# A decoder kernel: the last layer's norms and stores inside its steps, the first q and k beside the cross attention

## The chip, the cores and the metric

The kernel runs on one core of a Trainium2 chip. The metric is the device time of one execution in microseconds (us); less is better. Everything is fp32.

## The reference

The input is eight sequences of 256 tokens with 128 features, and a context of the same shape. A state-space block (Mamba style) is followed by a layernorm; then comes one cross attention with 16 heads, residual and layernorm; then six layers of windowed self attention with feed-forward; the result is added to the input of those layers and normalised:

```python
# stage 1 (b: 8, s: 256, d: 128): x1 = layernorm(x + ssm(layernorm(x)))
# stage 2: x2 = layernorm(x1 + cross_attention(layernorm(x1), layernorm(ctx)))
# stage 3, six times:
def attn_layer(x, Wqkv, qs, ksc, Wo):
    q, k, v = split(shift_tokens(x) @ Wqkv)      # 16 heads of 64
    q, k = l2norm(q) * qs, l2norm(k) * ksc
    q, k = rotary(q, scale), rotary(k, 1 / scale)
    return local_attention(q, k, v) @ Wo         # windows of 32, one window back
def ffn_layer(x, g, bln, W1, b1, W2, b2):        # x = shift_tokens(x)
    xn = layernorm(x) * g + bln
    a, gate = split(xn @ W1 + b1)                # 341 wide each
    return a * gelu(gate) @ W2 + b2
# x3 = x2; per layer: x3 += attn_layer(x3); x3 += ffn_layer(x3)
# out = layernorm(x3 + x2)
```

## The kernel before

Activations lie with the 128 features on the partitions. A pair of sequences (512 columns) is the unit of stages 1 and 2 and of the feed-forward; a single sequence (256 columns) is the unit of the self attention.

**Layernorm** (`layernorm_steps`, L101 to L138) works across partitions, so PE takes the means: one matmul with a matrix of 1/128 gives the mean spread over all partitions (ln_mu, L104); DVE subtracts (ln_xc, L108); ACT squares (ln_sq, L110); four small matmuls give the variance of each token as one column for each 128 tokens (ln_var, L115); ACT computes the inverse root by Ln and Exp on those four columns (ln_rs); four matmuls spread it over the partitions again (ln_bc, L128); DVE multiplies (L135, or L137 and L138 with gain and bias). It is a generator: a caller can run it in pieces between other work. In `fine` form it yields after each matmul group.

**Order of the work.** DVE, ACT, POOL and the DMA-issuing SP get their orders from a scheduler, starting from program order. In stage 3 PE's order is the program's own (`manual_schedule`). ACT's table for Ln and Exp is loaded again after each gelu (`load_table`, L93 in the profile), and what needs it is held behind that load (`with_table`, L89).

**Pools.** Tiles come from pools; the program opens a new pool for a stage when that of the stage before is closed. Unless told otherwise, the first use of a new pool's tile waits until the old pool that lay in its place is free as a whole.

**Stage 1** (0 to 383 us) runs the state-space scan over four pairs. **Stage 2** (383 to 684 us) loops over four pairs, and in each over 16 groups of heads: scores (s_ps, L514), clip (DVE w, L520), exp (ACT w), sums, and products with v (o_ps, L533). Beside pair p run the layernorms and projections of pair p+1 (`project`), one piece for each iteration; beside pair 3 runs nothing. At a pair's end come y_ps (L566), the residual r (L570) and the layernorm into x2.

**Stage 3** (from 684 us) starts by loading constants (rot, mask), clearing the padded buffers of k (kz, on POOL) and of v (three vz, on DVE), and loading weights: three thirds of wqkv, the scale rows from which DVE makes the rotary tables (`load_table3`, L610 and L616), wo, w1 and w2. Then it runs 48 steps, six layers by eight sequences. The list `slots` says what PE does in one step `run(n)`, for sequence n and, ahead of it, for n+1, n+2 and n+3: `shift` copies the input with the shifted half (xs, L654 and L655); `query_key` makes q or k of half a sequence (qk_ps L663; square L675; products with the tables qk L682 and rb L683; the two adds on POOL L686; sum of squares L687); `root` and `normalise` scale it (L706); `turn` transposes it and puts it down as qT or kz (L713 to L725); `value` copies v, from where DMAs place it in vz (L744); `scores` (L760 to L774), `weigh`, `add_weights`, `turn_weights` (pT_ps, L791), `attend` (L803), `turn_output` (L822) and `project_out` (y_ps, L835; x, L840) do the attention. The first two calls, `run(-2)` and `run(-1)`, fill this pipeline.

The feed-forward of a pair (`feed_forward`, L847 to L896) starts once both its sequences are through. Its pieces run in the "ff" slots of the next two steps. Of the eight "ff" slots in the list, a step n uses those whose number is n % 2; the others pass empty:

```python
if f == "ff":
    if k == n % 2:
        next(ff, None)
```

After step 47 follow the rest of its attention (`project_out`), the feed-forward of pair 3, and then, for the four pairs one after the other, the sum with x2 (L949), the layernorm, and `store` (four transposes st_ps L161, a copy st_o L163, a DMA).

## Time and profile before

| | |
|---|---|
| median of 3 runs | 2500.81 us (2500.76 to 2501.01) |
| the profiled execution itself | 2499.94 us |
| its span in the trace | 2498.2 us |
| busy share of the span: PE, DVE, ACT, POOL | 92%, 72%, 59%, 57% |
| mean granted clock of PE | 0.969 |

The busy share is a mean over stages with different limits. The page cuts the span into 40 slices of 62.5 us and gives the busy share of each in tenths; "PEclk" is the granted clock in tenths. PE reads 6 to 8 in stage 1 (slices 1 to 6), 9 in stage 2 with 8 at its end (slice 11), 7 where stage 3 begins, 9 through its steps, and 6 in the last slice. DVE reads 7 to 8 through the steps of stage 3.

Three views are used below. The windows give busy time by engine for a stretch of the span. The chain of waits follows the work that ended last back through what released it, printed in order of time. The timeline lists the instructions of a stretch. A number such as "x8" is the count of instructions in a group; "L128" is a line of the kernel.

### The profile page before, as it was taken

To read this page: it belongs to the slowest core of one execution; us is meant where nothing else is said; L and a number is where in the kernel's file an instruction comes from. 1 tells how busy PE (TensorE), PEld (TensorE's weight loads), DVE (VectorE), ACT (ScalarE), POOL (GpSimd) and SP (SyncE) were. 2 spreads that over 40 slices of the span, in tenths; PEclk is the share of its full clock that TensorE was granted. 3 is DMA by queue.
4 is the path that set the end of the run, shared out by engine and by line. 5 is a ranking of instruction groups with operands and counts; after the bars stand their busy time and mean duration, and the time that the engine had idled before them with its cause. 6 is when DMAs were issued, how large, how long until landed. Compare 5 with 4: busy or idle time off the path is not lost.

```text
span 2498.2 us, 54483 instructions
## 1 busy us (share of the span) xinstructions
PE 2310.4 (92%) x21378; PEld 1456.9 (58%) x21378; DVE 1795.9 (72%) x2661; ACT 1462.7 (59%) x2400; POOL 1432.0 (57%) x1180
## 2 busy tenths in 40 slices
PE   7688789999879999999999999999999999999996
PEld 3233235554446666666666666666666666666664
DVE  4788874444477777777777778777777877777762
ACT  4444444444446666666666666666666666666652
POOL 3889882222367665665656656666655666656630
PEclk9898899999979999999999999999999999999997
DMA  4444430000032223222222223222232223222220
GB/s 125 96 112 108 100 76 5 5 1 1 1 111 65 56 64 72 68 62 59 71 65 69 60 56 82 65 66 56 64 73 62 68 54 75 56 56 56 58 56 17
DMA packets 437963, 154.62 MB, mean 62 GB/s; under 512 B 401295, under 2 KB 417549, under 8 KB 437581
## 3 DMA queue, kind: packets, MB, share of 16 engines
q1 hardware_dynamic: 437708, 151.14, 25.0%
q8 instruction: 171, 2.80, 0.5%
q14 instruction: 84, 0.68, 0.1%
HBM read 55.33 MB, written 1.31 MB: 23 GB/s over the span
## 4 chain that ended last, share of the span: by engine, by line
PE 43%; DVE 32%; ACT 14%; POOL 4%; issue 3%; DMA 2%; SPq 1%; ACTq 0%; DVEq 0%; POOLq 0%
DVE qk L682 6%; DVE rb L683 6%; PE qk_ps L663 6%; DVE ss L687 6%; PE f_ps L869 3%; PE o_ps L803 3%; DVE on L810 3%; PE qkT_ps L713 3%; PE f_ps L894 2%; ACT sq L675 2%; PE s_ps L514 2%; PE o_ps L533 2%; DVE m L423 2%; POOL mc L425 2%; PE y_ps L835 2%
## 5 line engine op out<-in xcount | busy, mean ns | idle before, releaser
L686 POOL TENSOR_TENSOR qk<-qk,rb 128x512 f32<-128x512 f32 x384 | 481.0, 1274 | 434.4 <-DVE rb L683 288.3
L706 POOL TENSOR_TENSOR qk<-qk,rn 128x1024 f32<-128x1024 f32 x192 | 369.3, 1924 | 31.9 <-ACT rn L89 29.4
L682 DVE TENSOR_TENSOR qk<-qk_ps,tab 128x1024 f32<-128x1024 f32 x192 | 234.9, 1223 | 207.3 <-ACT sq L675 207.3
L663 PE MATMUL qk_ps<-wqkv,xs 128*128 128x512 f32 x768 | 373.7, 610 | 7.8 <-issue 3.1
L774 POOL TENSOR_TENSOR pw<-pw,mx 128x512 f32<-128x512 f32 x192 | 200.5, 1044 | 160.4 <-DVE mx L773 106.7
L725 ACT COPY kz<-qkT_ps 64x1024 f32<-64x1024 f32 x192 | 193.4, 1007 | 119.5 <-PE qkT_ps L713 117.5
L803 PE MATMUL o_ps<-vz,pT 128*32 128x128 f32 x6144 | 207.5, 276 | 29.7 <-ACT pT L795 27.1
L687 DVE TENSOR_REDUCE ss<-sq 128x16 f32<-128x1024 f32 x192 | 232.0, 1208 | 4.0 <-ACT sq L675 4.0
L683 DVE TENSOR_TENSOR rb<-qk_ps,tab 128x1024 f32<-128x1024 f32 x192 | 233.1, 1214 | 1.5 <-POOL qk L686 1.5
L783 DVE TENSOR_REDUCE mx<-pw 128x8 f32<-128x512 f32 x192 | 130.7, 681 | 140.9 <-ACT pw L89 138.7
L720 ACT COPY qT<-qkT_ps 128x1024 f32<-128x1024 f32 x96 | 97.2, 1013 | 218.7 <-PE qkT_ps L713 218.2
L803 PEld LDWEIGHTS o_ps<-vz,pT 128*32 128x32 f32 x6144 | 156.0, 109 | 118.3 <-ACT pT L795 107.2
L675 ACT ACTIVATE sq<-qk_ps 128x1024 f32<-128x1024 f32 x192 | 195.5, 1018 | 44.2 <-PE qk_ps L663 39.4
L713 PE MATMUL qkT_ps<-ident,qk 128*128 128x128 f32 x1536 | 211.1, 281 | 6.8 <-POOL qk L706 4.1
L523 POOL TENSOR_TENSOR ws<-w 128x512 f32<-128x512 f32 x64 | 81.4, 1272 | 216.5 <-ACT w L89 138.7
L760 PE MATMUL s_ps<-kz,qT 128*32 128x128 f32 x6144 | 203.1, 273 | 0.0
L406 PE MATMUL y<-mc,ident 128*128 128x512 f32 x256 | 153.3, 707 | 49.0 <-POOL mc L425 47.8
L663 PEld LDWEIGHTS qk_ps<-wqkv,xs 128*128 128x128 f32 x768 | 134.6, 195 | 106.3 <-issue 103.0
L713 PEld LDWEIGHTS qkT_ps<-ident,qk 128*128 128x128 f32 x1536 | 166.0, 142 | 47.8 <-issue 41.3
L835 PE MATMUL y_ps<-oT,wo 128*128 128x128 f32 x1536 | 187.7, 275 | 1.5 <-DVE ln_xc L108 0.9
L663 PE MATMUL v_ps<-wqkv,xs 128*128 128x512 f32 x384 | 181.7, 595 | 0.0
L835 PEld LDWEIGHTS y_ps<-oT,wo 128*128 128x128 f32 x1536 | 179.2, 192 | 2.2 <-DVE ln_xc L108 1.1
(155 smaller groups left out, 4358.4 us busy)
## 6 DMA issues: line engine op xcount, KB each, us to landing
vz<-v SPq DMA_DIRECT2D x1152, 64.0 KB, 2.2
rows<-bc_dram SPq DMA_DIRECT2D x128, 256.0 KB, 4.1
vz<-v SPq DMA_DIRECT2D x576, 32.0 KB, 2.4
wqkv<-in_L_ffn_Wqkv SPq DMA_DIRECT2D x18, 512.0 KB, 4.4
wo<-in_L_ffn_Wo SPq DMA_DIRECT2D x6, 512.0 KB, 7.1
w<-in_L_ffn_W SPq DMA_DIRECT2D x6, 341.0 KB, 3.3
t_in<-in_x SPq DMA_DIRECT2D x4, 256.0 KB, 3.8
wkv<-in_L_xattn_Wkv SPq DMA_DIRECT2D x1, 1024.0 KB, 8.1
```

Source lines behind the costliest of these rows:

```text
L663: T.matmul(pr[:, i * 512 : (i + 1) * 512], lhsT=got[n]["xs"][:, tb * P : (tb + 1) * P], rhs=thirds[seq[n][0], c][:, i * 512 : (i + 1) * 51 ...
L675: A.activation(sq, p3, AF.Square)
L682: V.tensor_tensor(t, p3, cs, ALU.mult)
L683: V.tensor_tensor(rb, p3, sn, ALU.mult)
L686: G.tensor_tensor(t[:, :, o], t[:, :, o], rb[:, :, f], ALU.add)
L687: V.tensor_reduce(got[n]["ss"][:, 2 * c + tb, :], sq, AX.X, ALU.add)
L706: G.tensor_tensor(t, t, r, ALU.mult)
L713: T.transpose(t_ps[:, hb * P : (hb + 1) * P], t[:, 2 * hb : 2 * hb + 2, :].rearrange("p h d -> p (h d)"), ident,)
L760: T.matmul(s_ps[i * W : (i + 1) * W, j * P : (j + 1) * P], lhsT=qT[:, 4 * g + i, j * W : (j + 1) * W], rhs=kz[:, 4 * g + i, :, k0 : k0 + 2 ...
L774: G.tensor_tensor(pw, pw, mx[:, 0].unsqueeze(3).to_broadcast(shape), ALU.subtract)
L803: T.matmul(o_ps[i * W : (i + 1) * W, j * P : (j + 1) * P], lhsT=pT[:, j, i * W : (i + 1) * W], rhs=vz[:, j, i].rearrange("p e d -> p (e d) ...
L835: T.matmul(y_ps[:, :P], lhsT=wts[d][0][:, hb, :], rhs=got[n]["oT", wh][:, hb, :], start=(hb == 0), stop=(hb == NHB - 1),)
```

## The change

1. **Layernorm.** A new argument `wide`, true by default: the variance comes from one matmul of the same matrix of 1/128 with all columns of the squares, so that it lies on all partitions; Ln and Exp work on all columns, and the spreading matmuls are gone. Only the feed-forward of a whole pair keeps the former way. Layernorms accept fewer columns. `fine` layernorms have one yield less.
2. **Pools.** The PSUM pool of stages 2 and 3 and the SBUF pools of both wait for the earlier users of a place tile by tile (`reuse_waits="tile"`), not for a whole pool. The pool with stage 2's inputs is closed before pair 3, and two pools of stage 3 open in its place.
3. **The first q and k.** `begin()` takes the place of `project` beside pair 3: the loads of stage 3's first weights and tables, `shift(0)`, and q and k of sequence 0. What it has done is left out of the slots later (`done`), and the calls of `run` begin at -1. The layernorm of pair 3's x2 runs in the "ff" slots of `run(-1)`. The three vz are cleared on POOL.
4. **The end.** `finish` adds x2, normalises, transposes and stores one pair or one sequence. In the last layer the free "ff" slots take it (`ends`, `queue`): pair 0 in step 44, pair 1 in step 46. Pair 3's feed-forward is done by sequence; that of its first one starts in step 47. After step 47 the second sequence's feed-forward alternates with what is queued, pair 2's finish included, and the last finish is that of the last sequence.

```diff
-    def layernorm_steps(x, dst, g=None, b=None, view=lambda t: t, fine=False):
+    def layernorm_steps(x, dst, g=None, b=None, view=lambda t: t, fine=False, wide=True):
...
-        var = ps_s("ln_var")
-        for j in range(4):
-            T.matmul(
-                var[:, j : j + 1], lhsT=sq[:, j * P : (j + 1) * P], rhs=mean_w[:, 0:1],
-                start=True, stop=True,
-            )
...
+        if wide:
+
+            var = ps_s("ln_var")[:, :n]
+            T.matmul(var, lhsT=mean_w, rhs=sq, start=True, stop=True)
+            if fine:
+                yield
+            inv_root(sq, var, eps_t)
+            if not fine:
+                yield
+            bc = sq
+        else:
...
+    def feed_forward(d, p, b=None):
+
+        w1, w2 = wts[d][1:3]
+        at = slice(0, TP) if b is None else slice(b * S, (b + 1) * S)
+        m = at.stop - at.start
+        x = x3[p][:, at]
+        if b == 0:
+
+            t0, t1 = (pools3["w"].tile([P, INNER], FP, tag="wqkv", name="fw", bufs=4) for _ in range(2))
+            xs, hh = t0[:, :m], t0[:, m : 4 * m]
+            xn, gts = t1[:, :m], [t1[:, (1 + j) * m : (2 + j) * m] for j in range(3)]
...
+        yield from layernorm_steps(xs, xn, col("ff_g", d), col("ff_b", d), wide=b is not None)
...
+    def finish(p, b=None):
+
+        at = slice(0, TP) if b is None else slice(b * S, (b + 1) * S)
+        x = x3[p][:, at]
+        m = at.stop - at.start
+        V.tensor_tensor(x, x, x2[p][:, at], ALU.add)
+        yield from layernorm_steps(x, x)
+        yield
+        tp = ps_s("st_ps")[:, :m]
+        for j in range(m // P):
+            T.transpose(tp[:, j * P : (j + 1) * P], x[:, j * P : (j + 1) * P], ident)
+        ot = pools3["w"].tile([P, INNER], FP, tag="wqkv", name="st_o", bufs=4)[:, :m]
+        A.copy(ot, tp)
+        o = out[2 * p : 2 * p + 2] if b is None else out[2 * p + b : 2 * p + b + 1]
+        nc.sync.dma_start(
...
+    def run(n):
+        nonlocal ff
+        for f, k, *args in slots:
+            if f == "ff":
+                next(ff if k == n % 2 else end, None)
+            elif 0 <= n + k < len(seq) and (f, n + k, *args) not in done:
+                f(n + k, *args)
+                if f is project_out and k < 0:
+                    d, b = seq[n + k]
+                    last = d == DEPTH - 1
+                    if b % 2:
+                        ff = feed_forward(d, b // 2)
+                    elif last and b == B - 2:
+                        queue.extend((feed_forward(d, b // 2, 0), finish(b // 2, 0)))
+                    if last and b % 2 and b > 1:
+                        queue.append(finish(b // 2 - 1))
+
+    def begin():
+
+        for name in ("w", "a"):
+            pools3[name] = ctx.enter_context(
+                tc.tile_pool(name=f"s3{name}", bufs=2, side="right", reuse_waits="tile")
+            )
+        fixed3["rot"] = pools3["w"].tile([P, 4, 2, HD], FP, name="rot", bufs=1)
+        nc.sync.dma_start(out=fixed3["rot"], in_=a["c_rot"])
+        for c in range(3):
+            load_third(0, c)
+        load_table3(0)
+        load(0)
+        yield
+        steps = [(shift, 0)]
+        for c in range(2):
+            for tb in range(2):
+                steps += [(query_key, 0, c, tb), (root, 0, c, tb), (normalise, 0, c, tb)]
+        for f, *args in steps:
+            f(*args)
+            done.add((f, *args))
+            yield
...
-            ahead = project(p + 1, nxt) if p + 1 < NPAIR else iter(())
+            if p == NPAIR - 1:
+                right2.close()
+            ahead = project(p + 1, nxt) if p + 1 < NPAIR else begin()
...
-            layernorm(r, x2[p])
+            if p < NPAIR - 1:
+                layernorm(r, x2[p])
+            else:
+                ff = layernorm_steps(r, x2[p])
...
-        for t in vzs:
-            V.memset(t, 0.0)
+        for t in fixed3["kzs"] + fixed3["vzs"]:
             G.memset(t, 0.0)
...
-            for n in range(-2, len(seq)):
+            shift(1)
+            for n in range(-1, len(seq)):
                 run(n)
             project_out(len(seq) - 1, 1)
-            for _ in feed_forward(DEPTH - 1, NPAIR - 1):
+            tail = feed_forward(DEPTH - 1, NPAIR - 1, 1)
+            queue.append(finish(NPAIR - 2))
+            while queue:
+                next(tail, None)
+                next(end)
+            for _ in tail:
+                pass
+            for _ in finish(NPAIR - 1, 1):
                 pass
-        for p in range(NPAIR):
-            V.tensor_tensor(x3[p], x3[p], x2[p], ALU.add)
-            layernorm(x3[p], x3[p])
-        store(x3)
```

## Prediction, on record before the run

> **What bounds the kernel now.** I read the slices of the page first (which engine is full, and when), then windows of single stages, then the chain of waits around the three places that the change touches: the border of stages 1 and 2, that of 2 and 3, and the end. The windows (columns: window, length, busy PE, PEld, DVE, ACT, POOL, granted clock, DMA share, GB/s):

> ```profile
> 400.00:460.00 60.00, 60.00 (x320) 30.05 (x321) 25.49 (x32) 30.68 (x51) 15.27 (x12) 1.00 0.00 1
> 630.00:680.00 50.00, 44.53 (x326) 25.13 (x326) 24.63 (x32) 26.98 (x50) 20.34 (x16) 1.00 0.00 1
> 690.00:700.00 10.00, 7.60 (x15) 3.38 (x13) 5.19 (x9) 2.04 (x4) 0.72 (x5) 0.57 1.01 311
> 1200.00:1400.00 200.00, 192.43 (x2156) 131.84 (x2155) 155.22 (x235) 131.61 (x214) 119.48 (x97) 0.99 0.29 69
> 2440.00:2470.00 30.00, 22.25 (x75) 13.16 (x73) 8.32 (x13) 8.43 (x14) 0.00 (x0) 0.78 0.00 0
> 2470.00:2499.00 29.00, 15.93 (x70) 11.34 (x68) 4.13 (x6) 5.64 (x13) 0.00 (x0) 0.74 0.12 37
> ```

> PE is full in stage 2 while it has projections beside it (400 to 460). In the last pair (630 to 680) it is not: nothing runs beside the attention. It is nearly full in stage 3's steady part, 1692 us long. Between, the work is a chain at a reduced clock. Two borders stand out. The cross attention's last y_ps ends at 683.8, and the first pT_ps of step 0 starts at 737.7: 53.9 us in which the pipeline of six layers fills. And the last y_ps of step 47 ends at 2442.15, the span at 2498.2: 56.1 us of feed-forward, four layernorms and the transfer. In the chain of waits (start, length, what):

> ```profile
> 683.78 0.76 DVE r L570
> 687.45 5.73 DMA wqkv<-in_L_ffn_Wqkv
> 693.32 3.76 PE qk_ps L663 x4
> ```
> ```profile
> 2442.15 0.30 DVE x L840
> 2446.33 1.88 PE ln_var L115 x8
> 2448.79 2.09 PE ln_bc L128 x8
> 2452.22 6.68 PE f_ps L869 x10
> 2465.54 1.07 PE ln_var L115 x8
> 2467.19 2.08 PE ln_bc L128 x8
> 2489.32 1.69 PE st_ps L161 x8
> 2491.65 2.42 DMA out<-st_o
> ```

> The first fill starts with a transfer of weights; the tail is one instruction at a time, everything waiting for the one before.

> **Part 1, layernorm.** Removed: four L128 matmuls, about 1.1 us at full clock (2.09 in the tail). The four L115 become one 128x512, like ln_mu's (1.02 to 1.14[...]), against 0.98 now: even. Ln and Exp (0.27+0.21) become 128x512; nearest row, the Exp of scores on 512 columns, 0.63 each: +0.8. So 1.1 to 2.1 us less PE, 0.8 more ACT, 0.3 to 1.3 less of a lone chain. Stage by stage:
> - First layernorm[...]: -1.
> - Stage 1's middle: POOL and DVE bound (slices 2 to 5 show POOL at 8 to 9), so the gain is covered. But the order on ACT changes: two more pairs of table loads there, 4x1.28 us, ACT being at 4 tenths. I take -1, with -6 to +6.
> - Border to stage 2: the first s_ps (383.10) waits until DVE's L135 (382.36, 0.70) has released the whole old pool, and behind ln_bc (380.69, 1.65). After, it waits for its own banks: -3.
> - Stage 2, pairs 0 to 2: PE full, so PE time is worth its length: six layernorms beside the attention at -1.0, three between pairs at -0.3: -7 (-4 to -10).

> **Part 2, first q and k beside the last cross-attention pair.** An iteration there is a chain in order on DVE and ACT: two iterations are the 5.97 us from 652.01 to 657.98.

> ```profile
> 652.01 1.23 DVE w L520
> 653.26 1.06 ACT w L89
> 655.13 1.08 PE o_ps L533 x8
> 657.98 1.23 DVE w L520
> ```

> Added to it: weights and tables (on SP's queue, where nothing of stage 2 stands behind them; only DVE's table and the first query_key wait for them), 12 steps with 4 query_keys, one step an iteration. A query_key is PE 1.88, ACT 1.02, DVE 1.22+1.22+1.21 and 0.16, POOL 2.5+1.9. Three iterations now take 8.94 with DVE some 4.6 busy and PE 7.5; after, DVE 8.3 and PE 9.4. If these filled ideally it would be 9.4 per group; but DVE is in order, and a block of 3.6 us in front of a clip of w holds ACT and PE. I take 10.5 (ends 9.4 and 12.5): 4x1.55 = +6.2. The scale table (DVE, 1.3) is +1.3, the lost layernorm of the next context -1, a possible stall of DVE's table on its DMA +0 to 4 (rows: 5.7 us for a third of wqkv from issue to landing, 3.0 for a scale row, behind some 1 MB on that queue). Together +7 (+2 to +15).

> What it takes from the fill: from the last y_ps to the first pT_ps there remain r and layernorm of pair 3 (no longer in front of sequence 0's q and k, but k and q of sequences 1 and v follow), 3 query_keys instead of 7. Walking down PE's new order with the rows above: turn of q at 1, layernorm to 4.5 to 6.4, kz copies to 9.5, next query_key's sq at 10.5, rb at 12.9, the following block at 14.8, v 16.7, scores 17.8, turn of k 19.3, last qk 21.2, pT at 22 to 24. Before 53.9, so -31. POOL must clear kz (3.94) and now the three vz (1.76 each on DVE): 9.2 us before the first k is put down, from about when stage 2's buffers come free, tile by tile; covered while v and kz come at 9.5, the tightest cover here; uncovered it costs up to 3.

> [...] PEclk over 690 to 700 is 0.57. [...] by the row (0.57 to 0.70 up to 730) some 5 us of matmuls on the path take half as long again, 24. I take 23.

> Part 2 net: -31 + 7 = -24 (-15 to -32).

> **Part 3, end of the last layer.** Moved into the last steps: finish of pairs 0 and 1, half of pair 3's feed-forward. In steps of a full PE they cost their PE time: 2x2.2 (mu, var, 4 transposes) and 2.6 for mu, var and f_ps of 256 columns: +7. In-order ACT holds Ln+Exp+copy of 512 columns (1.9 us) between the softmax's exps; range +4 to +12. Their two output transfers go into SP's queue among the vz copies of L744 (2.2 to 2.4 us each to landing); the next step's attend needs those a step later, so 0. Before, these four layernorms cost 6.6 us each in the tail (2464 to 2489.3), with 5.4 for storing.

> The tail after: feed-forward of 256 columns, each of the 512-column rows halved (mu 0.6, var 0.6, f_ps 3.4, f2 1.5, DVE and ACT pieces 0.4 each, no L128), 10.7 with its hand-overs, 2 to 3 more for the first half's rest that alternates with it: 13. finish of pair 2 stands on PE's queue ahead of the last one: 6. Last finish of 256 columns: mu 0.6, var 0.6, transposes 0.85, six others of 0.4: 5. Then copy to end of span as now, 3.4. In all 27 (25 to 33) against 56.1: -29.

> [...] Two gelus need ACT's table swapped twice: four loads in the tail instead of two. The trace prices a load at

> ```profile
> 2425.25 1.28 ACT L93
> ```

> [...] By the row the split costs +2.6 on ACT[...]; ACT hands the row's price straight on here (the exp starts 0.01 after the load), so I use it[...].

> **Part 4, steady part, pools.** Steps 0 to 43: per step 35.2 us ((2430 - 737.7)/48). The instructions' order and the kinds of their waits are unchanged on all five engines, and steady feed-forward keeps the narrow layernorm. Cost 0; what covers nothing is a different place of the buffers in memory, unknown: +-5.

> **Sum**, against the profiled execution (2499.94 us, span 2498.2): -1 -1 -3 -7 -24 +7 -29 = -58, so 2442. The median of the runs shown, 2500.81, is 0.9 above it: about 2443.

> **Rivals.**
> A. The attention's last pair stretches by nearly what the fill loses: DVE's in-order blocks, or the table waiting for the scale row behind the weights. For: DVE's clip opens every iteration of that chain. Against: DVE has half its time free there. At +15 for the stretch and a fill of 38, part 2 gives -1 and not -24: 2466. Chance 0.17.
> B. The end gives less: finish's Ln and Exp stand in front of an exp that PE waits for in steps 44 to 47 (+12 and not +7), finish of pair 2 runs strictly before the last one at half clock (33)[...]: 2443 + 5 + 6 + 2 = 2456. For: PEclk 0.74 to 0.78 there. Against: PE has other work beside most of it. Chance 0.2.
> C. Slower. The steady step itself gets longer: the buffers of wqkv, xs, qk and rb lie in pools on the other side of the memory now, and POOL works on qk and rb beside DVE 48x8 times. Place: qk L686, whose 2.5 us stand between rb L683 and the turn. From 58/48 = 1.2 us per step (3% of 35.2) the gain is gone; at 1.3 it is 2506. For: POOL's adds idle most behind rb L683 (288 us). Against: same order, same waits, and PE is 96% full with its own work. Chance 0.03.
> D. Stage 1 gets longer by 10 through the extra table loads in front of ab (ACT 0.69 ahead of the scan): 2453. Chance 0.06.
> That it does not do what it says: the q and k of sequence 0 land after the last y_ps all the same, since each engine is in order and their weights arrive late; that is A in full.

> **How the numbers follow.** My forecast, faster by the sum: 0.54 (2443, own range 2430 to 2455); A 0.17, B 0.2, D 0.06, C 0.03. The parts' ends added crosswise give 2424 to 2468, which holds A, B and D. A difference under 0.2%, 5 us, is what a measurement of this kernel can hardly tell from none. For that the gain would have to shrink to a tenth: 0.01. Slower: 0.03. Faster: 0.96.

> **What would show it.** Right: first s_ps of stage 2 about 3 us sooner after dn_ps; pairs 0 to 2 shorter by 7; qk_ps between iterations of the last pair, which takes some 7 longer; from its y_ps to the first pT_ps 21 to 26 us; steps at 35.2; from the last y_ps to the end 25 to 33, with half-size f_ps and no L128. Wrong: a step over 35.4; an idle DVE or PE of several us on the scale row's transfer; a fill over 30; the ACT table loads of stage 1 on the chain ahead of the scan.

## The result, and the profile after

The changed kernel takes 2460.51 us (median of 4 runs, 2459.99 to 2462.53) against 2500.78 (4 runs, 2498.28 to 2501.01): a ratio of 0.9843, 95% interval 0.9826 to 0.9860. It is faster by 40 us. The forecast was 2443. The result lies on the side that was forecast and inside the wide range of 2424 to 2468, but outside the narrow one of 2430 to 2455 that went with the sum: it falls 17 us short. The profiled execution took 2460.15 us, its span is 2458.4.

The span can be cut at five instructions that both traces have: the first s_ps of stage 2, the end of y_ps of pair 2, that of pair 3, the first pT_ps of step 0, the end of the last y_ps of step 47. All in us:

| stretch | before | changed | difference | forecast |
|---|---|---|---|---|
| start to first s_ps (stage 1 and border) | 383.1 | 399.2 | +16.1 | -5 |
| first s_ps to end of y_ps, pair 2 | 242.7 | 232.2 | -10.5 | -7 |
| to end of y_ps, pair 3 | 57.9 | 65.1 | +7.1 | +7 |
| to first pT_ps (the fill) | 54.0 | 21.4 | -32.6 | -31 |
| to end of last y_ps (48 steps) | 1704.4 | 1709.3 | +5.0 | +7 |
| to end of span (the tail) | 56.1 | 31.1 | -25.0 | -29 |
| sum | 2498.2 | 2458.4 | -39.8 | -58 |

18 us of the sum are missing. The first line is wrong in sign, by 21 us; the tail is 4 short; stage 2, the fill and the steps give 7 back. The windows of the changed kernel (window, length, busy PE, PEld, DVE, ACT, POOL, granted clock, DMA share, GB/s):

```profile
2427.00:2443.00 16.00, 12.32 (x51) 8.06 (x49) 6.55 (x16) 11.20 (x19) 0.00 (x0) 1.00 0.00 0
2443.00:2459.00 16.00, 6.14 (x13) 2.54 (x12) 2.23 (x4) 4.21 (x8) 0.00 (x0) 0.55 0.11 33
690.00:700.00 10.00, 8.56 (x29) 3.94 (x26) 1.86 (x3) 2.44 (x4) 3.47 (x1) 1.00 0.01 2
700.00:720.00 20.00, 15.64 (x114) 8.51 (x114) 12.56 (x16) 13.41 (x19) 14.78 (x13) 1.00 0.32 59
640.00:690.00 50.00, 44.69 (x301) 22.89 (x299) 37.23 (x50) 29.15 (x56) 35.50 (x27) 1.00 0.02 7
1200.00:1400.00 200.00, 192.64 (x2179) 133.60 (x2178) 159.05 (x240) 129.72 (x216) 121.49 (x98) 1.00 0.35 70
400.00:460.00 60.00, 60.00 (x342) 30.02 (x340) 32.81 (x40) 34.60 (x55) 19.24 (x16) 0.97 0.02 5
```

The last pair of the cross attention (640 to 690) now has DVE and POOL at work, for no more of PE. In the fill (690 to 720) the clock is 1.00; it was 0.57 from 690 to 700, and 0.70 at most up to 730. The steady part is as it was. The tail has two halves: 16 us at full clock, and 16 us in which PE works 6 us, at a clock of 0.55.

The chain of waits at the fill (start, length, what) no longer has the transfer of weights, and pair 3's layernorm follows y_ps at once:

```profile
690.27 6.21 PE y_ps L976 x14
696.47 0.87 PE qkT_ps L615 x8
697.35 1.11 PE ln_mu L105 x2
```

At the end, the same view shows where the second half of the tail goes:

```profile
2441.53 0.49 DVE x L805
2442.07 1.14 PE ln_mu L105 x2
2444.63 2.09 PE ln_var L117 x2
2448.87 1.11 PE st_ps L818 x4
2449.98 0.87 PE ln_mu L105 x2
2451.80 1.23 PE ln_var L117 x2
2454.49 0.70 PE st_ps L818 x2
2455.21 0.37 ACT st_o L820
```

The feed-forward is done at 2442.0, 14.8 after the last y_ps. From 2442.07 to 2449.98 PE serves the finish of pair 2 alone, 7.9 us, and only then the finish of the last sequence.

Then stage 1. In it, conv is a convolution on PE, xm its Silu on ACT, ab the decay of the scan (an Exp on ACT), m the scan on DVE, mc the scan's product on POOL, gate a second Silu on ACT, and dn_ps the matmul group that ends a pair. The timeline of pair 1 (start, length, engine, line, what; in brackets how long the engine had been idle, and what ended that) shows, in the changed kernel:

```profile
152.88 1.28 ACT L324 ACT_TABLE_LOAD   x1
158.74 8.18 PE L316 MATMUL conv<-xn,w_tap 128*128 128x512 f32 x16
163.53 0.69 ACT L324 ACTIVATE xm<-conv,cols 128x512 f32<-128x512 f32 x1 [9.37 <-PE conv L316]
166.96 0.69 ACT L324 ACTIVATE xm<-conv,cols 128x512 f32<-128x512 f32 x1 [2.75 <-PE conv L316]
167.67 1.28 ACT L93 ACT_TABLE_LOAD   x1
168.96 1.30 ACT L89 ACTIVATE ab<-dt,aa 128x512 f32<-128x512 f32 x2
169.68 2.42 DVE L420 TENSOR_TENSOR_SCAN m<-dw,ab 128x256 f32<-128x256 f32 x4 [7.89 <-ACT ab L89]
171.08 1.26 POOL L422 TENSOR_TENSOR mc<-m,rows 128x512 f32<-128x512 f32 x1 [12.90 <-PE d_ps L342]
```

and before:

```profile
158.96 1.28 ACT L327 ACT_TABLE_LOAD   x1
160.26 0.69 ACT L327 ACTIVATE xm<-conv,cols 128x512 f32<-128x512 f32 x1
162.60 0.69 ACT L327 ACTIVATE xm<-conv,cols 128x512 f32<-128x512 f32 x1 [1.66 <-PE conv L319]
170.21 1.26 POOL L425 TENSOR_TENSOR mc<-m,rows 128x512 f32<-128x512 f32 x1 [4.67 <-issue]
```

ACT loads the table for Silu at 152.9, six us before conv starts, and sits there until 163.5. Every ab stands behind it, so DVE's scan starves, then POOL's mc. Bracket by bracket: ACT 9.4 us for conv, DVE 7.9 for ab, POOL 12.9. Before, the table was loaded at 159.0, when the first half of conv was in, and xm followed at once; POOL's wait was 4.7. The "PE d_ps" named behind POOL's 12.90 is only the last releaser in the view's reckoning; the line that was late is DVE's m, and behind it ACT's ab. Pair 2 has the same (POOL 11.2 us, 4.7 before), pair 3 does not.

### The profile page after: what moved, and what is told of

Its sections match the earlier page's. It is cut to its first block, busy times and chain, and to the rows that moved or that the text cites. A ratio compares the mean times of both kernels' runs of the same rounds, so it can differ in the third digit from the quotient of the medians.

```text
span 2458.4 us, 53845 instructions
## 1 busy us (share of the span) xinstructions
PE 2268.2 (92%) x21054; PEld 1407.0 (57%) x21054; DVE 1788.4 (73%) x2668; ACT 1491.1 (61%) x2418; POOL 1439.4 (59%) x1184
## 4 chain that ended last, share of the span: by engine, by line
PE 36%; DVE 31%; ACT 15%; POOL 3%; issue 2%; DMA 1%; SPq 1%; ACTq 0%; POOLq 0%; DVEq 0%
DVE qk L584 6%; DVE ss L589 6%; DVE rb L585 6%; PE qk_ps L565 5%; PE f_ps L780 3%; PE o_ps L705 3%; ACT sq L577 3%; PE f_ps L804 3%; DVE on L712 3%; PE qkT_ps L615 2%; DVE mx L685 2%; PE v_ps L565 2%; ACT kz L627 2%; PE s_ps L662 2%; PE s_ps L922 2%
## 5 line engine op out<-in xcount | busy, mean ns | idle before, releaser
L565 PE MATMUL qk_ps<-wqkv,xs 128*128 128x512 f32 x768 | 364.2, 597 | 1.3 <-ACT qT L622 1.1
L420 DVE TENSOR_TENSOR_SCAN m<-dw,ab 128x256 f32<-128x256 f32 x256 | 160.6, 670 | 47.7 <-POOL mc L422 27.8
L422 POOL TENSOR_TENSOR mc<-m,rows 128x512 f32<-128x512 f32 x128 | 162.2, 1268 | 48.2 <-PE d_ps L342 24.1
L615 PEld LDWEIGHTS qkT_ps<-ident,qk 128*128 128x128 f32 x1536 | 164.9, 141 | 42.5 <-issue 40.7
```

Of the source, the lines that this page charges most:

```text
L565: T.matmul(pr[:, i * 512 : (i + 1) * 512], lhsT=got[n]["xs"][:, tb * P : (tb + 1) * P], rhs=thirds[seq[n][0], c][:, i * 512 : (i + 1) * 51 ...
L615: T.transpose(t_ps[:, hb * P : (hb + 1) * P], t[:, 2 * hb : 2 * hb + 2, :].rearrange("p h d -> p (h d)"), ident,)
```

## The experiments

### Does the order on ACT cost stage 1, or the wide layernorm?

Two things changed in stage 1 at once: the variance is wide, and a `fine` layernorm pauses twice and not three times, so all that comes behind it in the list of pieces (conv, Silu, d_ps, gate) moves up by one place among the scan's instructions.

**e1** puts the pause back:

```diff
             inv_root(sq, var, eps_t)
-            if not fine:
-                yield
+            yield
             bc = sq
```

> The changed kernel with one pause put back: the fine layernorm yields three times again (between Exp and the product), so that the pieces behind it in stage 1 come one step later; the wide form stays. Theory S (order on ACT): in the changed kernel Silu's table load and the two xm stand further ahead on ACT, wait there for conv (9.4 us) and hold the scan's ab; with the pause back the last dn_ps starts at 373 +- 2 us as before (390.4 changed) and the whole takes 2444 +- 3 us. Theory W (width): Ln and Exp over 512 columns and the wider variance hold the scan; then dn_ps stays at 388 to 391 and the time at 2458 to 2461.

Measured: 2441.08 us (2438.99 to 2443.46), ratio to before 0.9764 (0.9749 to 0.9778). The last dn_ps group starts at 374.3 (390.4 changed, 373.0 before). POOL's long wait in pair 1 is 4.69, as before. The wide form alone is not the cause, which is what theory S said.

**e2** takes the same pause out of the kernel before, and leaves the variance narrow:

```diff
                 start=True, stop=True,
             )
-        if fine:
-            yield
         if g is None:
```

> The kernel before with one edit: the fine layernorm's third pause is taken out; its variance stays narrow (four small matmuls, Ln and Exp on 4 columns). Theory S: stage 1 gets 15 to 18 us longer by the order alone, 2516 +- 3 us, with POOL idle about 12 us ahead of one mc in pairs 1 and 2. Theory W: no change, 2500 +- 2 us.

Measured: 2511.24 us (2510.65 to 2511.93), ratio 1.0044 (1.0029 to 1.0059). One `yield` less, no other edit, and the kernel is 10 us slower: the last dn_ps group starts 11.5 us later. That is less than the 15 to 18 expected. POOL's wait is shorter than in the changed kernel:

```profile
155.44 7.14 PE L317 MATMUL conv<-xn,w_tap 128*128 128x512 f32 x16 [0.16 <-DVE xn L136]
166.74 1.27 POOL L423 TENSOR_TENSOR mc<-m,rows 128x512 f32<-128x512 f32 x1 [8.34 <-issue]
```

Conv starts at 155.4 here and at 158.7 in the changed kernel, and takes 7.1 us and not 8.2. The 11.5 us do not all lie where those of the changed kernel lie. From the dn_ps of one pair to that of the next, pairs 1 and 2 together lose 15.6 us in the changed kernel (164.9 before, 180.5), 6.9 in e2 and 2.5 in e1; the rest of e2's loss is in the first pair and, 3.4 us, in pair 3. So in these two pairs the order alone carries 6.9 us and the wide form alone 2.5, and the other 6 appear only where the two meet. What the traces show of that remainder is a conv that starts later and runs at a granted clock of 0.88 (150 to 160 us; 1.00 in e2), while ACT is waiting for it. Why conv starts 3 us later was not tested by itself.

**e3** leaves the changed layernorm as it is, and puts a pause between conv and Silu:

```diff
                 yield
             yield
+            if p:
+                yield
             for h in range(2):
                 m = sp.tile([P, TP], FP, tag=f"xm{h}", name="xm")
```

> The changed kernel with two pauses in its fine layernorm, but one more pause between the conv matmuls and Silu (pairs 1 to 3). Only what stands behind conv moves back by a step; the layernorm itself is as in the changed kernel. Theory S: it is the distance of Silu from conv that counts, so most comes back: stage 1 ends at 373 to 381, 2444 to 2452 us. Were it the place of the layernorm's own pieces (they stay early), 2458 to 2461 us.

Measured: 2446.2 us (2440.97 to 2448.6), ratio 0.9780 (0.9763 to 0.9796). POOL waits 8.28 us, between 4.69 and 12.90, and the last dn_ps group starts at 377.2. Of 17.4 us 13.2 come back, so the cost follows the place of Silu and of what stands behind it, not that of the layernorm's own pieces. ACT still waits 7.1 us for conv here (9.4 changed); DVE's scan then starves for 3.4 us and not for 7.9.

### What of the fill is due to begin(), what to the pools?

**e5** runs begin behind the last pair:

```diff
-            ahead = project(p + 1, nxt) if p + 1 < NPAIR else begin()
+            ahead = project(p + 1, nxt) if p + 1 < NPAIR else iter(())
...
     early2.close()
+    for _ in begin():
+        pass
```

> The changed kernel, but begin (loads, shift, q and k of sequence 0) runs behind the last pair's attention and not beside it. If the cross attention's last pair carries it as the traces say (65.1 us against 57.9 before, fill 21.4 against 54.0), the pair goes back to 57 to 58 and the fill, with the weights' transfer (about 10 us until they land) and four query_key blocks of 3.6 us in front, to 44 to 48: +17 to +19, 2477 to 2480 us. If most of the fill's gain came from the pools' waits tile by tile or the layernorm in run(-1), the fill stays under 35 and the time under 2468.

Measured: 2473.08 us (2472.16 to 2475.18), ratio 0.9886 (0.9872 to 0.9901). Pair 3 is back at 58.0, the fill is 41.5: 20.1 us longer than in the changed kernel, 7.1 won in the pair, net 13. The time is under the 2477 to 2480 expected: the mechanism is as expected, the fill 3 to 6 us shorter than I had worked out. The place of begin thus carries 20 of the fill's 32.6 us; the other 12 are what e5 still has of the change (no `run(-2)`, the layernorm in `run(-1)`, the clearing on POOL, and perhaps the pools); it was not taken apart further.

**e7** is e1 with all pools waiting for whole pools again (`reuse_waits="tile"` removed in five places).

> e1 with the pools waiting for the whole pool before them again, in stages 2 and 3 (PSUM and SBUF). If tile by tile opens both borders: from the last dn_ps of stage 1 to the first s_ps 10 us or more again (7.9 in e1), and the fill of stage 3 longer by 3 to 10, as kz, vz and the first xs wait for all of stage 2: 2446 to 2455. If the pools' waits are hidden: 2440 to 2443.

Measured: 2446.34 us (2445.31 to 2450.09), ratio 0.9783 (0.9767 to 0.9800), against e1's 0.9764 (0.9749 to 0.9778): the intervals overlap. The time would fit the expectation that tile by tile opens both borders (2446 to 2455), but the stretches speak against it. The fill is 21.5 in both, so tile by tile gives the fill nothing. From the last dn_ps to the first s_ps it is 8.6 against 7.9 (10.1 before), not the 10 or more expected: most of what that border won comes from the layernorm, not from the pools. Pair 3 is 66.3 against 65.1. What is left of the difference between the medians I can't place.

### What does the end cost, and what does it give?

**e6** puts the end behind step 47 again, with everything else as changed. It is not quite the end of before: each `finish` still transposes and stores its own pair, where the kernel before stored all four pairs after the last layernorm.

```diff
-                next(ff if k == n % 2 else end, None)
+                if k == n % 2:
+                    next(ff, None)
...
+            for _ in feed_forward(DEPTH - 1, NPAIR - 1):
+                pass
+            for p in range(NPAIR):
+                for _ in finish(p):
+                    pass
```

> The changed kernel, but the end as before: no finish and no half feed-forward in the last layer's steps, the whole feed-forward of pair 3 and then four finishes one after the other behind step 47 (wide layernorm, pools and begin as changed). By the traces: the steps get back their 5 us (1704 to 1705 from the first pT_ps to the last y_ps), the tail is that of before less four times about 1.3 us for the wide form, 50 to 52 (31.1 changed): +14 to +16, 2475 to 2477 us. If finish in the steps cost nothing (PE had room), the steps stay at 1709 and it is 2480.

Measured: 2480.98 us (2478.51 to 2481.18), ratio 0.9914 (0.9900 to 0.9929). The steps take 1702.5, so finish and the half feed-forward cost 6.8 us in them; that the total equals the 2480 expected for "the steps stay at 1709" is chance. The tail is a surprise: 56.1, as long as before and not 50 to 52, though four times four ln_bc matmuls of 2.08 us are gone. The chain before goes from ln_bc straight to the ln_mu of the next pair:

```profile
2472.07 1.07 PE ln_var L115 x8
2473.71 2.08 PE ln_bc L128 x8
2475.79 1.53 PE ln_mu L104 x2
```

and in e6:

```profile
2448.20 1.72 PE ln_mu L105 x2
2451.34 2.09 PE ln_var L117 x2
2453.45 0.70 ACT ln_sq L89
2454.17 0.64 ACT ln_sq L89
2454.84 0.70 DVE x L142
2455.58 1.12 PE st_ps L818 x4
2456.70 1.72 PE ln_mu L105 x2
2459.85 1.14 PE ln_var L117 x2
```

Three things took the place of ln_bc. Ln and Exp on all columns take 1.34 us where they took 0.48. The product and the four transposes of a pair (0.70 and 1.12) now stand in front of the next pair's ln_mu; that is the order of `finish`, which the expectation leaves out. And the matmuls are slower: ln_mu took 1.38 to 1.57 in the tail before, ln_var 1.07. The granted clock in this window is low:

```profile
2440.00:2476.00 36.00, 17.80 (x35) 6.54 (x33) 6.87 (x10) 10.12 (x16) 0.00 (x0) 0.61 0.10 29
```

**e9** tests what the clock costs by giving PE work of no use:

```diff
         T.matmul(mu, lhsT=mean_w, rhs=x, start=True, stop=True)
+        if warm:
+            T.matmul(ps_o("warm"), lhsT=mean_w, rhs=x, start=True, stop=True)
...
             T.matmul(var, lhsT=mean_w, rhs=sq, start=True, stop=True)
+            if warm:
+                T.matmul(ps_o("warm"), lhsT=mean_w, rhs=xc, start=True, stop=True)
```

> e6 with one 128x512 matmul more after ln_mu and one after ln_var in each of the four finishes; their results are not used. e6's tail was 56.1 us, as long as before, though the wide form took the four ln_bc (2.08 us) out of each finish; its granted clock there was 0.61 (0.74 before), and ln_mu took 1.72 and ln_var 2.09. If the missing work on PE lowers the clock and so eats the gain, then with PE fed again the clock is 0.8 or more, ln_mu and ln_var take about 1.1, and the tail 50 to 53 us in spite of eight matmuls more. If the clock is low for another reason (a chain of small matmuls whatever PE does), the tail stays at 56 or grows to 60.

Measured: 2473.76 us (2472.52 to 2474.59), ratio 0.9891 (0.9877 to 0.9906). Eight matmuls more, and the tail is 49.8 us and not 56.1, shorter than the lower end of what I expected:

```profile
2436.00:2471.00 35.00, 23.75 (x62) 9.25 (x61) 8.93 (x13) 13.23 (x20) 0.00 (x0) 0.99 0.10 30
```

PE is busy 68% of the window at a clock of 0.99; in e6 it was 49% at 0.61. From one ln_mu to the next it is 6.2 us here, 8.5 and 7.6 in e6, 6.5 and 6.7 before. The low clock thus costs e6 some 6 us; the product and the transposes are still on the chain.

**e10** takes the changed kernel and steps the finish of pair 2 beside the last feed-forward:

```diff
-            queue.append(finish(NPAIR - 2))
+            other = finish(NPAIR - 2)
             while queue:
                 next(tail, None)
                 next(end)
+                next(other, None)
             for _ in tail:
-                pass
+                next(other, None)
+            for _ in other:
+                pass
```

> The changed kernel with e4's end alone (finish of pair 2 beside the last feed-forward), stage 1 as changed. By the traces of e1 and e4 (tails 30.2 and 26.2) the tail goes from 31.1 to 26 to 27 and nothing else moves: 2455 to 2457 us. If e4's gain over e1 was a difference between runs, 2459 to 2461.

Measured: 2456.11 us (2455.56 to 2456.58), ratio 0.9822 (0.9805 to 0.9838): the tail is 26.5 (31.1 changed), the rest as in the changed kernel, as expected.

### The best of both

**e4** is e1 with that end.

> e1 and one more edit at the end: finish of pair 2 is stepped beside the last feed-forward and the other queued work, not behind it. In the changed kernel it takes 7.9 us alone (2442.07 to 2449.98) at a granted clock of 0.55, and its input is there at 2425.8. If its place is the cost, 6 to 8 us less than e1: 2437 +- 3. If PE's clock and ACT's table loads set the end anyway, its matmuls only push the feed-forward back: 0 to 3 us less than e1, 2441 to 2444.

Measured: 2438.49 us (2437.76 to 2439.89), ratio 0.9754 (0.9739 to 0.9768). That is 2.6 us under e1; the tail is 26.2 against e1's 30.2, so the place of pair 2's finish is worth 4 us, less than the 6 to 8 expected. What is on the chain runs at full clock but for the last 9 us (0.73 from 2428 to 2437):

```profile
2429.42 0.71 PE ln_mu L105 x2
2431.08 0.71 PE ln_var L117 x2
```

**e8** adds the narrow layernorm inside stage 1 to e4.

> e4 with the narrow layernorm, three pauses, inside stage 1 (pairs 1 to 3 and the first projection; the first layernorm and the last of stage 1 stay wide). In e1 the pairs of stage 1 are 0.5 to 1.9 us longer each than before, which would be the wide form's Ln and Exp (0.8 us more on ACT each): if so, stage 1 gets 2 to 4 us shorter, 2435 +- 2. If these us are the layernorms' other order alone: same as e4, 2437 to 2440.

Measured: 2441.02 us (2437.31 to 2442.0), ratio 0.9754 (0.9740 to 0.9769), the same as e4's. Its profiled run has stage 1 at 379.5 (382.9 in e4), but that run was the fastest of the four. Inconclusive: if there is something in it, it is under what these runs tell apart. e4 stands as the version to keep, 22 us under the changed kernel.

## Why the prediction was right, and where it was wrong

- **Layernorm, stage 2.** Forecast -7, measured -10.5. From one y_ps to the next it is 81.85 us before and 77.80 now, for three layernorms: 1.35 us each, not 1.0 for two of them and 0.3 for the third. PE was busy 81.14 us and is now 77.33: the ln_bc are gone in full (3.5 us for each pair), and the variance costs about the same (3.2 and 3.4). The mis-sized term is above all the layernorm between the pairs, which lies beside matmuls too.
- **Layernorm, lone chains.** Forecast 0.3 to 1.3 less of each. No run measures this alone: in e6 `finish` also changes the order, and the clock falls (0.61 from 2440 to 2476). The lines give 2.08 us of ln_bc gone and 0.86 more of Ln and Exp, as forecast; what the forecast did not price is the matmul at a low clock: ln_var took up to 2.09 in e6, against 1.07 before.
- **Stage 1's middle.** Forecast -1, range -6 to +6; measured +17.4 at the last dn_ps. This step failed. It priced the change in ACT's order by what ACT executes (two pairs of table loads, ACT at 4 tenths) and not by what ACT waits for at its new place. Rival D (+10) had the place right and the cause wrong. Its four extra loads are there: 22 table loads in stage 1 in the changed kernel and in e2, against 18 before, in e1 and in e3. But they split gate, where POOL then waits 1.0 and 1.2 us in pairs 1 and 2 against some 0.5 before; Silu's wait for conv costs POOL 8.2 and 6.5 us more.
- **Border to stage 2.** Forecast -3, measured -1.3 from the last dn_ps to s_ps (10.1 to 8.8), -2.2 in e1. The forecast put it down to the release of the old pool and to ln_bc; with whole pools (e7) 1.5 of e1's 2.2 remain, so the pools are the smaller part.
- **Last pair.** Forecast +7 from 10.5 us for three iterations; measured +7.1. The chain shows 10.87 from one rb to the next (654.73, 665.60, 676.47), which by the forecast's own sum would make +8: part of the agreement is luck. The table's wait for its transfer (0 to 4) did not come on top. Rival A is out.
- **Fill.** Forecast -31 with 22 to 24 us left; measured 21.4, so the lower number, with nothing added for a low clock, was the right one: the clock reads 1.00 from 690 to 720. The 5.73 us transfer of weights does not by itself explain the low clock before: PE had other work during it (busy 2.07 of the 3.41 us from 688.40), its longest waits in that fill were 3.05 and 3.26 us, and the clock fell at 688.4 us, when no wait of the fill had yet been over 1.5 us:

```profile
684.99:688.40 3.41, 1.77 (x10) 0.97 (x8) 2.09 (x2) 1.08 (x3) 1.82 (x1) 1.00 0.22 36
688.40:691.81 3.41, 2.07 (x8) 1.78 (x8) 2.61 (x3) 2.21 (x7) 2.32 (x5) 0.50 0.86 270
702.68 3.75 PE L663 MATMUL qk_ps<-wqkv,xs 128*128 128x512 f32 x4 [3.05 <-issue]
720.19 1.97 PE L713 MATMUL qkT_ps<-ident,qk 128*128 128x128 f32 x8 [3.26 <-POOL qk L706]
```

That 22 us came out is in part luck; the last section has what went with a low clock. POOL's clearing of kz and vz is nowhere in the chain.
- **Last layer's steps.** Forecast +7; e6 gives 6.8.
- **Tail.** Forecast 27, measured 31.1. The term that failed is the finish of pair 2, 6 us: it took 7.9 at a clock of 0.66 (2442.07 to 2449.98), and the feed-forward ended at 14.8 and not at 13. e10 shows that its place alone cost 4.6. Rival B had this half of its story right (33 us), not the other: 12 us in the steps.
- **Steady part.** Forecast 0; in e6, without finish, the steps take 1702.5 against 1704.4. Rival C is out. The 35.2 us a step of the prediction came from an end at 2430 us; to the last y_ps it is 35.5 before and 35.6 changed, so its sign "a step over 35.4" tells nothing.
- **Table loads.** The row's 1.28 us was the right price: in the tail the load ends at 2429.73 and gelu starts 0.01 us later. In stage 1 before, ACT ends an ab at 158.94, the load starts at 158.96 and xm at 160.26: 0.02 us on either side of the load.

```profile
2428.45 1.28 ACT L793
2429.73 0.01 issue
2429.74 0.84 ACT fw L793 x2
```

With stage 1 repaired (e1, 2441 us) the forecast of 2443 would have been met, by errors that cancel: stage 2 and the fill better, stage 1 and the tail worse.

## What to carry to other kernels

An engine that works in order is charged for what it waits for, not for what it does (in pair 1 ACT's table load took 1.28 us, its wait for conv 9.37, and the next ab, behind both, held DVE for 7.89): when a change moves an instruction up by a place, look at the time when its input is there, and at what stands behind it. A pause that seems to belong to one helper also sets the place of everything after it; after removing one, compare the order on every engine, not its busy share. And where PE does little, its clock can be low (0.61 in e6's end, PE busy 49%; 0.55 in the last 16 us of the changed kernel, PE busy 38%): read the granted clock before pricing a chain of small matmuls, and try to move such a chain beside other work (e10, 4.6 us) before trimming it. When you take a test kernel "back" to an old order, check on the chain that it is the old order.

## What the runs showed of the hardware that I had not expected

Whether the low clock goes with the share of busy time or with the length of the gaps, e6 and e9 don't tell apart, since the added matmuls shorten the gaps too. The traces of the two kernels say more. The shortest time at one clock in either is 3.41 us; three stretches of that length in a row, in stage 1 of the kernel before, and PE's wait in the first of them:

```profile
186.64:190.05 3.41, 1.71 (x4) 0.68 (x4) 3.41 (x2) 1.44 (x2) 2.64 (x3) 1.00 0.16 50
190.05:193.47 3.42, 1.40 (x3) 0.30 (x2) 3.42 (x7) 1.78 (x3) 2.27 (x2) 1.00 0.35 111
193.47:196.88 3.41, 2.97 (x3) 1.00 (x4) 3.41 (x6) 2.56 (x4) 3.41 (x4) 0.50 0.00 0
188.34 1.13 PE L406 MATMUL y<-mc,ident 128*128 128x512 f32 x2 [2.32 <-POOL mc L425]
```

The first has a gap of 2.32 us, PE is busy 50% of it, and the clock stays at 1.00 in the next. The second has, up to its end, no gap over 1.3 us, PE is busy 41% of it, and in the third the clock is 0.50. Cut into stretches of 3.41 us from the first clock record on (22.80 us before, 7.45 in the changed kernel), the two traces have 41 at a clock of 1.00 with PE busy under half: in 31 cases the next one is at 0.50. Of 1324 with PE busy half or more, 12 are followed by one at 0.50. So in these two traces a low clock goes with little work on PE just before it, and the stretch with the longer gap kept its clock. They are stretches of two similar kernels, not independent trials; what the clock goes by, and what the exceptions have in common, was not shown.
